# Attention mask in a diffusion block: from an added matmul to a product on VectorE, with the sums over keys one stage later

## The chip, the cores and the metric

The kernel runs on one core of a Trainium2 chip. The core has a matrix engine (TensorE, PE in the profile; its weight loads are PEld), three engines for elementwise work (VectorE or DVE, ScalarE or ACT, GpSimd or POOL) and a queue engine (SyncE or SP) that issues most DMAs here. TensorE writes to PSUM[...]; everything else lies in SBUF. The metric is the device time of one execution in microseconds; the time of the kernel before is the median of three runs.

## The reference

The input is x, 32 sequences of 256 tokens with 256 features, and a condition per sequence. A conditional state-space block is followed by two layers of attention and feed-forward, and the input is added at the end. The change concerns the attention alone:

```python
def local_attention(q, k, v):                      # WINDOW = 128, 8 heads of 64
    ...
    bk, bv = (look_around(bk), look_around(bv))    # each window also sees the one before
    sim = jnp.einsum('bhwid,bhwjd->bhwij', bq, bk)
    i = bt[:, :, None]
    j = btk[:, None, :]
    mask = (i < j) | (i > j + WINDOW) | (j == -1)
    sim = jnp.where(mask, -jnp.finfo(sim.dtype).max, sim)
    attn = jax.nn.softmax(sim, axis=-1)
    out = jnp.einsum('bhwij,bhwjd->bhwid', attn, bv)
```

So a query i sees the keys from i - 128 to i. For 256 tokens there are two windows of 128. Queries are l2-normalised and rotated before, as are keys; values are not.

## The kernel before

The 32 sequences go in four groups of eight. For each group a scan (the state-space block, `group_scan`) runs over 256 time steps, and two layers of attention and feed-forward follow. The scan of the first group runs alone. From then on the scan of the next group runs beside the two layers of the present one: `side_by_side` takes the attention and feed-forward as a sequence of pieces (each `yield` in `blocks` ends one) and gives out the 315 pieces of the scan evenly between them, about one and a half to a piece of attention. The last group has no scan beside it. Within this written order a scheduler settles the order on each engine; every engine then works in order, and semaphores tie the engines together.

The attention of one sequence is `blocks`' inner loop, eight pieces long. Sequence b is scored while sequence b+1 is already projected:

1. project v of the first window of b+1; turn (transpose) the second window of b
2. project q and k of the first window of b+1
3. `divide` b-1; scores of the second window's keys, all heads
4. scores of the first window's keys, half of the heads; project v of the second window of b+1
5. project q and k of the second window of b+1
6. scores of the first window's keys, the other half; output projection of b-1 (`finish`)
7. `sums` and `values` of b
8. turn of the first window of b+1

In the last two sequences of a layer, the pieces from the sixth on also carry the normalisation of the feed-forward's first input (`normalise`, `spread`).

A projection of q or k fills one PSUM bank (L736). `rotated` then works on it with all three elementwise engines: squares on ACT (L749), products with the rotation tables on DVE (L752, L757), sum of squares on DVE (L762, L766), the addition, the inverse root and the product with it on POOL (L760, L768, L769). `turn` transposes the result on TensorE (L775) and copies it with ACT (L780).

`scores` computes the transposed scores, keys on partitions. It fills two banks, one for the even and one for the odd heads. Each bank begins with a matmul that writes the mask into it (L934): the identity in bfloat16 times `mask_t`, which holds 0 where a key is seen and -32768 where not. The products of keys and queries (L941, 64 rows) accumulate onto it, and ACT takes the exponential of the whole bank (L950) into a tile `pT` of 128x512, of which six exist; a sequence uses all six. No maximum is subtracted.

`sums` adds the exponentials over the keys with a matmul per head (L960, `rs`), and DVE takes the reciprocal (L968). `values` multiplies with v (L979) and ACT copies the result (L986). `divide` spreads the reciprocal over the heads' rows by a matmul (L994), and DVE multiplies (L1002). `finish` is the output projection (L786), which DVE adds to the residual (L794).

All PSUM tiles but one come from one pool of seven banks (`ps_w`), taken in turn, so a matmul that opens a bank waits until the reader of that bank's former content is done. There is also a second program in the file (`exact`), for inputs whose scores might be too large; it isn't executed here.

Of the kernel before, what the change touches and what calls it, by code (L numbers as in the profile page):

```python
# [10 lines left out]
FP = mybir.dt.float32  # L11
BF = mybir.dt.bfloat16
I32 = mybir.dt.int32
AF = mybir.ActivationFunctionType
ALU = mybir.AluOpType
# [4 lines left out]
P = 128  # L20
# [18 lines left out]
W = 128  # L39
# [4 lines left out]
LN_EPS = 1e-5  # L44
CLIP = 10.0
MASKED = -1e30
MASKED_LOW = -32768.0


SCALES2 = 25.0  # L50
# [2 lines left out]
def bc(ap, axis, n):  # L53

    ap = ap.unsqueeze(axis)
    shape = list(ap.shape)
    shape[axis] = n
    return ap.broadcast_to(shape)
# [15 lines left out]
def kernel(  # L74
# [29 lines left out]
    nc = tc.nc  # L104
# [4 lines left out]
    const = ctx.enter_context(tc.tile_pool(name="const", bufs=1))  # L109
# [27 lines left out]
    ident = const.tile([P, P], FP, tag="ident", name="ident")  # L137
# [15 lines left out]
    for j in range(NJ):  # L153
# [18 lines left out]


    mask_t = const.tile([P, 2 * W], BF, tag="mask_t", name="mask_t")
    ident_b = const.tile([P, P], BF, tag="ident_b", name="ident_b")
    nc.vector.tensor_copy(ident_b, ident)
    nc.gpsimd.memset(mask_t, 0.0)
    nc.gpsimd.affine_select(
        out=mask_t[:, 0:W], in_=mask_t[:, 0:W], compare_op=ALU.is_ge, fill=MASKED_LOW,
        base=0, pattern=[[1, W]], channel_multiplier=-1,  # L180
    )
    nc.gpsimd.affine_select(
        out=mask_t[:, W : 2 * W], in_=mask_t[:, W : 2 * W], compare_op=ALU.is_ge,
        fill=MASKED_LOW, base=0, pattern=[[-1, W]], channel_multiplier=1,
    )


# [5 lines left out]
    for h in range(HEADS):  # L193
# [7 lines left out]
        out=b1g_sb[DH : DH + MREM], in_=b1[0:MREM, :, 1, len(MCH) - 1]  # L201
# [12 lines left out]
    with tc.tile_pool(name="setup", bufs=2) as setup, tc.tile_pool(  # L214
        name="setup_ps", bufs=2, space=PSUM
    ) as sps:

        for src, pos, dst in ((qk_scale, rot_c, rc_sb), (qk_scale_sw, rot_s, rs_sb)):
            tab = setup.tile([P, NW, 2, DH], FP, tag="tab", name="tab")
            nc.scalar.dma_start(out=tab, in_=pos)  # L220
            for l in range(L):
                sc = setup.tile([P, 2 * DH], FP, tag="qk_sc", name="qk_sc")
                nc.scalar.dma_start(
                    out=sc, in_=src[l].rearrange("a d -> (a d)").partition_broadcast(P)
# [39 lines left out]
        for i in range(3):  # L264
            for src, k, dst in ((wx_sb, 0, wsum), (wx0, 1, wbias)):
# [3 lines left out]
                for c in range(NC_):  # L269
# [4 lines left out]
                        start=(c == 0),  # L274
                        stop=(c == NC_ - 1),
# [12 lines left out]
    def program(ctx, exact):  # L288
# [10 lines left out]
        ps_w = ctx.enter_context(tc.tile_pool(name="psw", bufs=7, space=PSUM, reuse_waits="tile"))  # L299
# [496 lines left out]
        if exact:  # L796
# [4 lines left out]
                out=mask[:, 0:W], in_=mask[:, 0:W], compare_op=ALU.is_ge, fill=MASKED,  # L801
                base=0, pattern=[[1, W]], channel_multiplier=-1,
            )
            nc.gpsimd.affine_select(
                out=mask[:, W : 2 * W], in_=mask[:, W : 2 * W], compare_op=ALU.is_ge, fill=MASKED,
                base=0, pattern=[[-1, W]], channel_multiplier=1,
# [94 lines left out]
        class Attention:  # L901
# [24 lines left out]
            def scores(self, b, kw, i0, n):  # L926


                qT, kT, _ = self.qkv[b]
                nq = S - kw * W  # L930
                banks = []
                for r in range(2):
                    sc = ps_w.tile([P, n, nq], FP, tag="w", name="sc")
                    nc.tensor.matmul(  # L934
                        sc, ident_b, bc(mask_t[:, 0:nq], 1, n), start=True, stop=False
                    )
                    banks.append(sc)
                for i in range(n):
                    for r in range(2):
                        rows = slice(r * DH, (r + 1) * DH)  # L940
                        nc.tensor.matmul(  # L941
                            banks[r][:, i, :],
                            kT[rows, i0 + i, kw * W : (kw + 1) * W],
                            qT[rows, i0 + i, kw * W :],
                            start=False,
                            stop=(i == n - 1),
                        )
                for r in range(2):
                    p = aw.tile([P, n, nq], FP, tag="pT", name="pT", bufs=6)
                    nc.scalar.activation(p, banks[r], AF.Exp)  # L950
                    for i in range(n):
                        self.p[b, kw, i0 + i, r] = p[:, i, :]

# [192 lines left out]
        def ff_weights(l):  # L1146
            return (
                weights(w1, l, [P, KM, 2 * HID], "w1_sb"),
                weights(w2, l, [P, len(MCH), DM], "w2_sb"),
            )  # L1150
# [29 lines left out]
        def blocks(g, at, nxt):  # L1180

            for l in range(L):
                ff = FeedForward(g, l, at.res, *ff_weights(l))
                for b in range(GB):
                    more = b + 1 < GB
                    more and at.project(b + 1, 0, 2)
                    at.turn(b, 1)
                    yield
                    more and at.project(b + 1, 0, 0)
                    more and at.project(b + 1, 0, 1)  # L1190
                    yield
                    b > 0 and at.divide(b - 1)
                    at.scores(b, 1, 0, HEADS // 2)
                    yield
                    at.scores(b, 0, 0, 2)
                    more and at.project(b + 1, 1, 2)
                    yield
                    more and at.project(b + 1, 1, 0)
                    more and at.project(b + 1, 1, 1)
                    yield  # L1200
                    at.scores(b, 0, 2, 2)
                    b > 0 and at.finish(b - 1)
                    if b >= GB - 2:
                        ff.normalise(0, 2 * (b - GB + 2))
                    yield
                    at.sums(b)
                    at.values(b)
                    if b >= GB - 2:
                        ff.normalise(0, 2 * (b - GB + 2) + 1)
                        ff.spread(0, 2 * (b - GB + 2))  # L1210
                    yield
                    more and at.turn(b + 1, 0)
                    if b >= GB - 2:
                        ff.spread(0, 2 * (b - GB + 2) + 1)
                    yield
                yield
                at.divide(GB - 1)
                yield
                res, follow = at.res, None

                def last(m):
                    nonlocal follow
                    if m == 0:
                        if l + 1 < L:
                            follow = Attention(l + 1, res, *attention_weights(l + 1))
                        else:
                            follow = nxt()
                    if follow is not None:
                        lead_in(follow, m)

                pieces = feed_forward(ff, last)
                next(pieces)
                at.finish(GB - 1)
                yield
                for _ in pieces:
                    yield
                at = follow
            state_at[0] = at
# [3 lines left out]
        for _ in group_scan(0, ys):  # L1242
            pass
        at = Attention(
            0, [load_res(ys, j) for j in range(GB // 2)], *attention_weights(0)
        )
        for m in range(6):
            lead_in(at, m)
        for g in range(NG):
# [12 lines left out]
            at = state_at[0]  # L1262
# [119 lines left out]
```

## Time and profile before

| what | value |
|---|---|
| median of three runs | 4266.41 us (4258.27 to 4266.48) |
| the profiled execution, its own time | 4264.77 us |
| its span, first to last instruction | 4262.5 us |
| mean granted TensorE clock | 0.963 |
| DMA queue of most transfers | 34.1% of 16 engines' span |
| scan of the first group, alone | the first 546 us |
| mask matmuls (L934) | 384, of 128x512 bfloat16, mean 383 ns |
| exponentials (L950) | 384, of 128x512, mean 590 ns |
| sums over keys (L960) | 2048 instructions |
| reciprocal (L968) | 64, mean 1751 ns |

In the profile's lines an instruction is told by its line in the kernel, its engine and operation, and the tiles that it writes and reads (out<-in). A group's line gives the number of instructions, their busy time in us and the mean of one in ns, and then the idle time of the engine just before them, with what ended it. A line of waits gives the waiting instruction, what it waited for, the total in us, how often and the longest. Matmuls are pipelined, so that the busy time of one is longer than the distance from its start to the next one's start.

### The profile page before, as it was taken

The page shows a single profiled execution, that of the slowest core. Times are in us where ns is not written, and L with a number is a line of the kernel's source. Part 1 is how long each engine was busy: PE and PEld are TensorE (multiplying, and loading weights), DVE is VectorE, ACT ScalarE, POOL GpSimd, SP SyncE. Part 2 cuts the span into 40 slices and gives each one's busy share as a digit, 9 for nine tenths or more (in the row PEclk, how much of TensorE's full clock was granted, in tenths as well). Part 3 has the DMA queues.
Part 4 walks back from the last instruction along what each step waited for, and adds up shares of the span by engine and source line. Part 5 has one row for each costly group of instructions (what it writes and reads, how often), then busy time and mean ns, then how long its engine had stood idle before and what let it go on. Part 6 is the DMA issues. An engine that isn't in the chain of part 4 may idle for free. (4 is left out here: it accounts for less than half of the span.)

```text
span 4262.5 us, 51606 instructions
## 1 busy us (share of the span) xinstructions
PE 3885.2 (91%) x17980; PEld 2003.9 (47%) x17980; DVE 2600.1 (61%) x4952; ACT 1744.2 (41%) x3217; POOL 1684.0 (40%) x1749
## 2 busy tenths in 40 slices
PE   5777799898898999999899999999989899999999
PEld 2222255544455445544455445554455544654653
DVE  5777557666676546766776645766677653443442
ACT  2554335443444334443444423544344433322331
POOL 3333165323553156422555126532355314523531
PEclk9899999999999999999999999999999999999999
DMA  5777603443334312443433521344333431000000
GB/s 150 178 185 180 155 24 85 119 104 105 92 92 120 100 57 56 111 108 94 115 95 96 140 67 39 85 119 104 105 95 90 127 95 51 1 20 21 1 10 31
DMA packets 266114, 386.30 MB, mean 91 GB/s; under 512 B 161779, under 2 KB 170996, under 8 KB 263668
## 3 DMA queue, kind: packets, MB, share of 16 engines
q1 hardware_dynamic: 261776, 380.86, 34.1%
q8 instruction: 145, 2.38, 0.2%
q10 hardware_dynamic: 4068, 2.04, 0.2%
q14 instruction: 125, 1.02, 0.1%
HBM read 347.70 MB, written 33.55 MB: 89 GB/s over the span
## 5 line engine op out<-in xcount | busy, mean ns | idle before, releaser
L543 ACT ACTIVATE xrep<-xrep,beta 128x512 f32<-128x512 f32 x1024 | 693.1, 715 | 929.2 <-DMA xrep<-xnd 797.2
L550 DVE CUSTOM_DVE_ANT_0 h<-h,xrep,lim 128x512 f32<-128x512 f32 x1024 | 916.4, 895 | 149.7 <-ACT xrep L543 58.5
L736 PE MATMUL ps_qkv<-wqkv_sb,res 128*128 128x512 f32 x1536 | 733.6, 616 | 16.9 <-DMA res<-ys 6.3
L760 POOL TENSOR_TENSOR rot<-rot,swp 128x512 f32<-128x512 f32 x256 | 331.1, 1293 | 586.8 <-DVE swp L757 503.5
L736 PEld LDWEIGHTS ps_qkv<-wqkv_sb,res 128*128 128x128 f32 x1536 | 287.5, 196 | 359.4 <-issue 303.3
L562 PE MATMUL y<-h,ly 128*32 128x512 f32 x2048 | 411.3, 632 | 48.9 <-DVE h L550 48.0
L768 POOL TENSOR_TENSOR rn<-ss,neg_half 128x8 f32<-128x8 f32 x256 | 434.2, 1696 | 26.5 <-DVE ss L766 14.1
L1087 PE MATMUL po_f<-ag,w_sb 128*128 128x512 f32 (+1 forms) x768 | 378.8, 617 | 37.8 <-DVE ag L1076 37.8
L752 DVE TENSOR_TENSOR rot<-ps_qkv,rc_sb 128x512 f32<-128x512 f32 x256 | 175.6, 686 | 369.2 <-ACT sq L749 369.0
L326 PE MATMUL ps_in<-xg,w_in_sb 128*128 128x256 f32 x1024 | 393.0, 517 | 1.8 <-DMA xg<-in_xT_dram 1.5
L1066 PE MATMUL pa<-hT,w_sb 128*128 128x512 f32 (+1 forms) x896 | 363.8, 596 | 0.0
L1076 DVE SCALAR_TENSOR_TENSOR ag<-pa,b_sb,gl 128x512 f32<-128x512 f32 x192 | 143.4, 747 | 329.9 <-PE pa L1066 210.3
L1066 PE MATMUL pg<-hT,w_sb 128*128 128x512 f32 x640 | 313.7, 613 | 0.0
L769 POOL TENSOR_TENSOR rot<-rot,rn 128x512 f32<-128x512 f32 x256 | 276.7, 1081 | 19.1
L326 PEld LDWEIGHTS ps_in<-xg,w_in_sb 128*128 128x128 f32 x1024 | 190.1, 199 | 187.4 <-issue 127.1
L1029 POOL TENSOR_TENSOR rstd<-ve,neg_half 128x1 f32<-128x1 f32 x128 | 76.5, 598 | 508.1 <-DVE ve L1027 494.5
L373 DVE SCALAR_TENSOR_TENSOR acc<-xr,wc_sb,acc 128x256 f32<-128x256 f32 x384 | 190.0, 506 | 126.7 <-POOL acc L362 122.7
L1087 PEld LDWEIGHTS po_f<-ag,w_sb 128*128 128x128 f32 (+1 forms) x768 | 141.6, 194 | 229.4 <-issue 143.6
L950 ACT ACTIVATE pT<-sc 128x512 f32<-128x512 f32 x384 | 206.2, 590 | 97.1 <-PE sc L941 96.4
L786 PE MATMUL ps_wo<-oT,wo_sb 128*128 128x256 f32 x1024 | 237.3, 385 | 0.0
L583 POOL TENSOR_TENSOR xd<-xd,dskip_sb 128x512 f32<-128x512 f32 x64 | 86.8, 1357 | 367.1 <-DMA xd<-xnd 202.4
L749 ACT ACTIVATE sq<-ps_qkv 128x512 f32<-128x512 f32 x256 | 148.9, 594 | 200.7 <-PE ps_qkv L736 147.5
(144 smaller groups left out, 5444.2 us busy)
## 6 DMA issues: line engine op xcount, KB each, us to landing
xrep<-xnd SPq DMA_DIRECT2D x512, 512.0 KB
xnd<-xn SPq DMA_DIRECT2D x64, 256.0 KB
xd<-xnd SPq DMA_DIRECT2D x256, 64.0 KB
wqkv_sb<-in_wqkv_dram SPq DMA_DIRECT2D x8, 1536.0 KB
w_sb<-in_w_dram SPq DMA_DIRECT2D x8, 1364.0 KB
xg<-in_xT_dram SPq DMA_DIRECT2D x64, 128.0 KB
ys<-yo SPq DMA_DIRECT2D x64, 128.0 KB
res<-ys SPq DMA_DIRECT2D x32, 256.0 KB
```

Of the source, the lines that this page charges most:

```text
L326: nc.tensor.matmul(ps, w_in_sb[:, k, ch * P : (ch + 1) * P], x, start=(k == 0), stop=(k == KM - 1),)
L543: nc.scalar.activation(bx, bx, AF.Copy, scale=ck[c]["beta"][:, t : t + 1])
L550: nc.vector._custom_dve(TENSOR_ADD_SAT, out=h_new, in0=state["h"], in1=bx, s0=ck[c]["lim"][:, 0, t : t + 1], s1=ck[c]["lim"][:, 1, t : t + 1],
L562: nc.tensor.matmul(ck[c]["y", hb][32 * q : 32 * q + 32, :], ly[hb % 2][:, 32 * t : 32 * t + 32], ck[c].pop(("h", hb * TB + t)), start=(i = ...
L736: nc.tensor.matmul(ps, res[b // 2][:, k, b % 2, t0 : t0 + W], wqkv_sb[:, k, a * DI : (a + 1) * DI], start=(k == 0), stop=(k == KM - 1),)
L760: nc.gpsimd.tensor_add(rot, rot, swp)
L768: nc.gpsimd.tensor_tensor(rn, ss, neg_half, ALU.pow)
L769: nc.gpsimd.tensor_mul(rot, rot, bc(rn, 2, DH))
L786: nc.tensor.matmul(po[:, d], wo_sb[:, c, d * P : (d + 1) * P], oT[:, c, :], start=(c == 0), stop=(c == NC_ - 1),)
L950: nc.scalar.activation(p, banks[r], AF.Exp)
L1066: nc.tensor.matmul(ps[0:n, :], self.w1[:, k, half_ * HID + o : half_ * HID + o + n], self.h[j][:, k].rearrange("p b t -> p (b t)"), start= ...
L1087: nc.tensor.matmul(self.po[d], self.w2[0:n, m, d * P : (d + 1) * P], self.ag[m][0:n, :], start=(m == 0), stop=(m == len(MCH) - 1),)
```

## The change

The mask is no longer added to the scores. `mask_t` now holds 1 where a key is seen and 0 where not. The products of keys and queries open their banks themselves, ACT takes the exponential of the unmasked scores, and DVE multiplies each tile `pT` in place with the mask, spread over the heads. The identity in bfloat16 and the copy that made it are gone. In `blocks`, the turn of the next sequence's first window moves ahead of `sums` and `values`, which come one piece later; the pieces of `normalise` and `spread` stay where they were.

```diff
     mask_t = const.tile([P, 2 * W], BF, tag="mask_t", name="mask_t")
-    ident_b = const.tile([P, P], BF, tag="ident_b", name="ident_b")
-    nc.vector.tensor_copy(ident_b, ident)
-    nc.gpsimd.memset(mask_t, 0.0)
+    nc.gpsimd.memset(mask_t, 1.0)
     nc.gpsimd.affine_select(
-        out=mask_t[:, 0:W], in_=mask_t[:, 0:W], compare_op=ALU.is_ge, fill=MASKED_LOW,
+        out=mask_t[:, 0:W], in_=mask_t[:, 0:W], compare_op=ALU.is_ge, fill=0.0,
...
                 for r in range(2):
-                    sc = ps_w.tile([P, n, nq], FP, tag="w", name="sc")
-                    nc.tensor.matmul(
-                        sc, ident_b, bc(mask_t[:, 0:nq], 1, n), start=True, stop=False
-                    )
-                    banks.append(sc)
+                    banks.append(ps_w.tile([P, n, nq], FP, tag="w", name="sc"))
                 for i in range(n):
                     for r in range(2):
                         rows = slice(r * DH, (r + 1) * DH)
@@
                             qT[rows, i0 + i, kw * W :],
-                            start=False,
-                            stop=(i == n - 1),
+                            start=True,
+                            stop=True,
                         )
                 for r in range(2):
                     p = aw.tile([P, n, nq], FP, tag="pT", name="pT", bufs=6)
                     nc.scalar.activation(p, banks[r], AF.Exp)
+                    nc.vector.tensor_mul(p, p, bc(mask_t[:, 0:nq], 1, n))
                     for i in range(n):
                         self.p[b, kw, i0 + i, r] = p[:, i, :]
@@
                     if b >= GB - 2:
                         ff.normalise(0, 2 * (b - GB + 2))
                     yield
-                    at.sums(b)
-                    at.values(b)
+                    more and at.turn(b + 1, 0)
                     if b >= GB - 2:
                         ff.normalise(0, 2 * (b - GB + 2) + 1)
                         ff.spread(0, 2 * (b - GB + 2))
                     yield
-                    more and at.turn(b + 1, 0)
+                    at.sums(b)
+                    at.values(b)
                     if b >= GB - 2:
                         ff.spread(0, 2 * (b - GB + 2) + 1)
                     yield
```

## The prediction

> **What bounds the kernel now.** I read the engine shares, then the windows by stage, TensorE's timeline where nothing else interferes, and last the groups and waits.
>
> ```profile
> PE 3885.2 (91%) x17980; PEld 2003.9 (47%) x17980; DVE 2600.1 (61%) x4952; ACT 1744.2 (41%) x3217; POOL 1684.0 (40%) x1749
> ```
>
> TensorE (PE) is busy for 91% of the span, VectorE (DVE) for 61%. The windows split this by stage (length, then busy time of each engine):
>
> ```profile
> core 0: us, PE busy (x) PEld busy (x) DVE busy (x) ACT busy (x) POOL busy (x), PEclk, DMA share, GB/s
> ...
> 546.00:819.00 273.00, 253.75 (x1533) 150.80 (x1532) 186.98 (x361) 125.18 (x238) 156.07 (x155) 0.99 0.27 73
> ...
> 1053.00:1377.00 324.00, 288.90 (x1688) 165.09 (x1686) 222.88 (x410) 149.58 (x285) 161.27 (x151) 0.96 0.39 99
> ...
> 3576.00:3778.00 202.00, 197.53 (x1278) 122.73 (x1277) 97.34 (x186) 79.20 (x142) 111.75 (x88) 0.99 0.03 9
> ```
>
> The first two are the attention of layer 0 and layer 1 beside the next group's scan. Such a pair comes three times, 48 sequences in all. The third is attention in the last group, with no scan beside it. That happens twice, for 16 sequences. With the scan, DVE is busy for 68 to 69% of the window and PE for 89 to 93%. Without it DVE has 48% and PE 98%. There PE's timeline repeats every 26.6 us:
>
> ```profile
> start us, us, engine line op out<-in xcount [idle before <-releaser]
> 3705.19 1.46 PE L994 MATMUL rb<-rinv,head_rows 128*128 128x256 f32 x6
> 3706.48 0.59 PE L934 MATMUL sc<-mask_t,ident_b 128*128 128x512 bf16 x2
> 3707.01 1.16 PE L941 MATMUL sc<-qT,kT 64*128 64x128 f32 x16
> 3708.10 0.61 PE L934 MATMUL sc<-mask_t,ident_b 128*128 128x512 bf16 x2
> 3708.64 1.14 PE L941 MATMUL sc<-qT,kT 64*128 64x256 f32 x8
> ```
>
> No row shows idle time before it: each pair of mask matmuls holds PE for 0.53 us from its start to the next row's start. Next the waits: what PE waits for in the whole span, then what DVE waits for in the layer 1 window (total, times, longest).
>
> ```profile
> PE tp_hn L1044 <- DVE hn L1031: 51.3, 28, 4.6
> PE rs L960 <- ACT pT L950: 49.1, 20, 8.5
> ...
> PE sc L934 <- DVE swp L757: 19.0, 17, 1.8
> ```
>
> ```profile
> DVE acc L373 <- POOL acc L362: 20.9, 10, 6.1
> DVE sg L593 <- ACT th_g L587: 20.0, 8, 5.6
> DVE rot L752 <- ACT sq L749: 13.3, 8, 3.1
> DVE hn L1031 <- POOL rstd L1029: 12.0, 4, 5.7
> ```
>
> PE's own waits in attention are few, and most name DVE or the exponentials. DVE, when idle, waits as often for POOL's round trips (acc, hn) as for PE's products (rot).
>
> **What the Trainium skill says.** "Perfetto Trace Analysis", Identifying the Most-Contended Engine, warns that matmul busy time is no fair measure of how near TensorE is to its limit. I therefore use starts of successive matmuls, not busy time. "TensorE: Matmul & The Clock Gate", Back-to-back issue gap, gives N/2.4 + 2.5 ns, or 216 ns for 512 columns. The first mask matmul of a pair is followed after 0.214 us here, so the trace agrees. "VectorE: DVE Perf Modes", The TRN2 errata, gives (N+151)/0.96 ns for an fp32 tensor_tensor, or 691 ns at 512 elements. The nearest row here, with one operand in PSUM, has 0.68 us. "SBUF — State Buffer", Who interferes with whom, says that a DVE instruction with two SBUF inputs contends with a GpSimd instruction that reads SBUF. The trace fits that: the scan step (two SBUF inputs) has a median of 0.81 us but a mean of 0.895, with single ones of 1.88. The new multiply is of this kind.
>
> **The change part by part.**
>
> *Mask matmuls removed.* 384 of them, in 192 pairs. The unmerged records show 0.214 us after the first of a pair and 0.308 after the second. The extra 0.09 is the step to the 64-row products, and it stays, because it will follow whatever matmul comes before. So a pair saves 0.43 us: 192 x 0.43 = 82.6 us, or 1.29 us per sequence. In the last group that is a plain gain, 16 x 1.29 = 21 us. In the 48 others (62 us) it counts only as far as PE still sets the pace.
>
> *Multiplies added.* 384 on DVE, each 128x512 with both inputs in SBUF. These bound one from below and above:
>
> ```profile
> L550 DVE CUSTOM_DVE_ANT_0 h<-h,xrep,lim 128x512 f32<-128x512 f32 x1024 | 916.4, 895 | 149.7 <-ACT xrep L543 58.5 <-PE y L562 40.1 <-DVE h L550 13.1
> ...
> L1002 DVE TENSOR_TENSOR oT<-oT,rb 128x512 f32<-128x512 f32 x128 | 86.7, 678 | 21.4 <-PE rb L994 19.0 <-ACT kT L780 2.4
> ```
>
> From below, the oT product has 0.68 us, of which neighbours overlap by 0.08, so 0.60. From above, the scan step's mean of 0.895. I take 0.70, the skill's figure plus a little contention: 269 us in all, 4.2 per sequence. DVE goes to about (187 + 34)/273 = 81% and (223 + 34)/324 = 79% in the two scan windows, and to 65% in the last group. In the last group its idle time, half the stage, covers the multiplies. With the scan only part is covered. Each multiply waits for its exponential, and behind it on DVE stand the next scan steps, the convolution, the gate, the residual sum and the reciprocal. PE waits for those through banks (swp 19.0, in other rows rinv 9.3, qkv on swp 5.1, oT 4.8) and through hn (51.3): 90 us in all. Bounds: no growth if the idle 31% covers everything. If waits grow like busy over idle (72 to 85% in a scan sequence: 2.6 to 5.7), 90 us becomes 195, or +105. I take half of the present sum again: +45.
>
> *Sums and values one stage later.* Before, PE waits 49.1 us for exponentials at the sums (73.5 counted by weight loads, which partly hide). Now the turn of the next sequence (8 transposes, 0.87 us) stands in between, and beside the scan mostly one or two scan pieces of 0.9 to 1.9 us too: about 2.5 us more cover. Against it stand two multiplies, 1.4 us, behind two rotation chains of about 2.3 us on DVE. In the last group DVE ends those chains 0.7 us after the second exponential, the multiplies would end at about 3719.9, and the sums start at 3720.2: no stall. With the scan I expect half of the 49.1 to go: -25. Bounds: -49, or 0 if DVE's queue replaces ACT's.
>
> *What moves with it, at nothing.* The turn needs POOL's rotated tiles. In the last group POOL has these 6.7 us before the sums' present start, which covers the earlier place; without that cover it would cost POOL's lateness, up to 3.6 us a time as in the present waits on rot. Its two ACT copies (0.59 us each) now precede the copies of values, with no DMA and nothing on SP or POOL moved. The reciprocal comes one stage later, but 2.75 us of value products and at least 5.2 of projections still stand ahead of its use. In the last two sequences of a layer one normalisation loses the cover of sums and values (1.44 + 2.75 us) and its neighbour gains it: even, within 8 us. The pT tiles live longer, yet all six are still freed before the next sequence's scores.
>
> *Sum.* -83 - 25 + 45 = -63. The profiled execution took 4264.8 us (span 4262.5), 1.6 below the median of 4266.4. So 4202 for it, 4203 against the median; I say 4205.
>
> **The rivals.**
>
> *DVE keeps up wholly* (0.20). All of PE's saving comes through and the sums stop waiting: 83 + 40 less 10 of new waits = -113, so 4153. For it: 31% idle DVE. Against it: DVE idles at points, in order, and can't be late for free.
>
> *Gain eaten, no change within 0.2%* (0.10). New DVE waits of 83 to 115 us, just inside the upper bound: 4258 to 4275.
>
> *DVE becomes the pace beside the scan: slower* (0.24). Its place is the six scan windows. If DVE's waits for POOL and ACT do not shrink when it has more to do, a window takes its busy time, plus these waits, plus 48 multiplies. In layer 1 the waits are 57 (acc, hn, stat, rhs, xc, h) and 20 (sg): 223 + 77 + 48 x 0.8 = 338 against 324. In layer 0 all waits but those on PE's products (rot, res, st) are 51: 187 + 51 + 38 = 276 against 273. Three times 14 and 3 is +51; less 21 in the last group +30, so 4296. With 0.895 a multiply it is +57, 4323. It decides from about 0.7 us a multiply if no wait shrinks. Against it: waits such as acc on POOL shrink when something else is placed in them, and the built order does place multiplies between the rotation chains and the convolution.
>
> That the mask matmuls do not really leave is no rival: the built order has no mask matmul, and 384 multiplies.
>
> **How the numbers follow.** My forecast, part of the gain survives, has 0.46, with its own range 4170 to 4240. The other cases have 0.20, 0.10 and 0.24. A measurement of this kernel tells about 0.2% from no change (the runs before spread by that): 8.5 us. Faster is 0.46 + 0.20, same 0.10, slower 0.24. The range that leaves out one in ten on each side reaches from 4148 (best case with a little more) to 4290 (a bit over half of the slow case).
>
> **What would show it.** Right: no mask rows; in the last group a sequence every 25.3 us instead of 26.6; multiplies of 0.65 to 0.8 us; waits of the sums below 49 us and naming DVE; waits on hn and swp up by some tens of us. Wrong: layer 1 windows as long as before or longer, with PE waiting for DVE at sums, y or banks; multiplies near 0.9 us; POOL's rotations much longer than their present 1.29 and 1.08 us, which would make the turns wait.

## The result, and the profile after

The changed kernel takes 4262.97 us (median of four, 4251.46 to 4268.31) against 4263.86 for the kernel before, measured beside it (4258.27 to 4266.48). The ratio is 0.9996, with a 95% interval of 0.9972 to 1.002. The forecast was 4205 and faster. What came is the rival with the lowest chance: the gain is eaten.

The profiled execution took 4268.31 us, its span is 4266.6. The page's engine line of the changed kernel:

```profile
PE 3842.9 (90%) x17596; PEld 1996.5 (47%) x17596; DVE 2907.0 (68%) x5335; ACT 1743.3 (41%) x3217; POOL 1762.5 (41%) x1749
```

The 384 mask matmuls are gone, and VectorE is busy for 307 us more. GpSimd, to which the change gives nothing, is busy for 78 us more. The windows of the changed kernel, cut from a layer's first scores to the first scores of its eighth sequence (layer 0 and layer 1 beside the scan), and seven sequences and a bit of the last group:

```profile
core 0: us, PE busy (x) PEld busy (x) DVE busy (x) ACT busy (x) POOL busy (x), PEclk, DMA share, GB/s
547.40:799.90 252.50, 223.34 (x1293) 133.16 (x1292) 202.31 (x365) 105.81 (x203) 156.10 (x146) 0.95 0.22 61
1071.40:1363.00 291.60, 259.38 (x1471) 149.00 (x1470) 241.23 (x420) 136.35 (x255) 165.94 (x145) 0.94 0.38 99
3591.00:3790.00 199.00, 189.57 (x1238) 120.09 (x1237) 135.74 (x235) 78.55 (x144) 119.88 (x89) 0.98 0.03 11
```

The same stretch of layer 0 took 236.7 us before and takes 252.5 now; that of layer 1 took 290.3 and takes 291.6; that of the last group's first layer took 183.2 and takes 177.8. Over whole layers (from first scores to first scores) the three layer-0 passes together grew by 37 us, the three of layer 1 shrank by 19 and the last group by 15. That this stretch of layer 1 is as long as before is what the prediction named as a sign against it. Of the 16 us in layer 0's stretch some 10 come with the new order alone (246.3 us in the first experiment below), and the rest of that layer gives 8 of them back; whole layers are the safer measure. VectorE is now at 80% and 83% of the scan windows (forecast 81 and 79).

The last group did what was forecast, and a little more. Its TensorE timeline in the changed kernel:

```profile
start us, us, engine line op out<-in xcount [idle before <-releaser]
3696.41 2.03 PE L934 MATMUL sc<-qT,kT 64*128 64x128 f32 x24
3698.37 5.42 PE L733 MATMUL ps_qkv<-wqkv_sb,res 128*128 128x512 f32 x12
...
3709.30 1.51 PE L954 MATMUL rs<-pT,head_cols 128*32 128x256 f32 x32
3710.74 2.82 PE L973 MATMUL ov<-pT,v_sb 128*64 128x256 f32 x32
...
3721.44 2.03 PE L934 MATMUL sc<-qT,kT 64*128 64x128 f32 x24
```

A sequence comes every 25.03 us (3696.41 to 3721.44) instead of 26.6, and no row of that steady stretch shows idle time. That is 0.5 us for each pair of mask matmuls, where the prediction took 0.43. The multiplies and the sums one stage later cost nothing there.

Now the multiply's own rows: the page's group line, then the tile view's counts and durations (minimum, median, maximum in ns):

```profile
L944 DVE TENSOR_TENSOR pT<-pT,mask_t 128x512 f32<-128x512 f32 x384 | 314.3, 854 | 36.2 <-ACT pT L943 36.1
```

```profile
L944 DVE TENSOR_TENSOR pT<-pT,mask_t x384: 658/683/1785, 550.1 to 4119.6; 128x512 f32<-128x512 f32 x192
```

The median is 683 ns, near the 691 that the prediction started from, but the mean is 854. The multiplies fall into two kinds: 282 of the 384 take 0.70 us or less, and 98 take 0.8 to 1.8. What GpSimd does at the time goes far to tell them apart. Of the 64 that start while it is in its product with the rotation (L757, 128x512), 55 are long, and the mean of the 64 is 1227 ns. The 88 that are overlapped by nothing but its inverse root on tiles of 128x8 (L765) have a mean of 682, the 44 that nothing of GpSimd overlaps 683. GpSimd pays too: its products with the rotation (L757, L766) rose from 1293 and 1081 ns to 1376 and 1119, and an L757 that a multiply overlaps has a mean of 1514, one without 1298. The Trainium skill, "SBUF — State Buffer", Who interferes with whom, states that a VectorE instruction with two SBUF inputs contends with a GpSimd instruction that reads SBUF. For the large products the trace agrees; beside the small one it shows no slowing.

The waits of TensorE in the whole span of the changed kernel (total us, times, longest; rows that changed little are left out):

```profile
...
PE sc L934 <- DVE swp L754: 48.1, 30, 3.3
...
PE tp_hn L1038 <- DVE mv L1019: 31.6, 5, 7.7
PE rs L954 <- DVE pT L944: 29.6, 25, 2.9
PE tp_hn L1038 <- DVE hn L1025: 27.6, 8, 7.2
...
PE tp_hn L1038 <- DVE ve L433: 13.4, 3, 4.7
```

Against the kernel before: the sums' wait for exponentials (49.1) has become 29.6 for the multiply; the scores' wait for a bank that VectorE frees went from 19.0 to 48.1; the turn of the normalised input (tp_hn) from 51.3 to 72.6 (31.6 + 27.6 + 13.4). All of TensorE's waits together grew by about 50 us.

Last the clock. The mean granted TensorE clock fell from 0.963 to 0.950. Windows of the changed kernel, one clock record (3.41 us) each, around one wait in layer 1, and the timeline there:

```profile
core 0: us, PE busy (x), PEclk, DMA share, GB/s
1297.05:1300.46 3.41, 2.38 (x30) 1.00 0.55 153
1300.46:1303.88 3.42, 1.20 (x5) 1.00 0.01 1
1303.88:1307.29 3.41, 3.41 (x7) 0.50 0.20 70
1307.29:1310.70 3.41, 3.41 (x14) 1.00 0.36 84
```

```profile
1302.68 1.13 PE L323 MATMUL ps_in<-xg,w_in_sb 128*128 128x256 f32 x4 [3.25 <-DVE res L791]
1303.64 3.38 PE L733 MATMUL ps_qkv<-wqkv_sb,res 128*128 128x512 f32 x4
1306.82 1.28 PE L772 MATMUL tr_qk<-ident,rot 128*128 128x128 f32 x8
```

TensorE waits 3.25 us for VectorE's residual sum. The record that holds most of this wait has 1.20 us of work; in the next record the clock is 0.50, and four projections take 3.18 us up to the next row's start. In the last group, where the clock is full, the same row of four takes 1.82 (3713.49 to 3715.31). So a wait is paid twice: once as idle time and again as slow work behind it, which costs up to 1.7 us in a record (half of 3.41). Many slow stretches are longer than one record: after the first scores they last 5.8 us in the mean.

To add this up, I split the time from the first scores to the end of the span into three: idle time (gaps that the profile counts as waits of TensorE), clock loss (half of the time at clock 0.5 in which TensorE is not idle), and the rest, which is TensorE's work at full clock, with gaps of less than 0.15 us, which aren't counted as waits.

| kernel | first scores to end | idle | clock loss | rest |
|---|---|---|---|---|
| before | 3715.9 | 226.3 | 91.2 | 3398.4 |
| after | 3719.2 | 276.7 | 127.1 | 3315.4 |
| difference | +3 | +50 | +36 | -83 |

TensorE's work fell by 83 us, the forecast's 82.6. The agreement is closer than the split is sharp: kernels below with the same matmuls as the changed one have a rest between 3302 and 3338. Waits and their slow clock took all of it back. Most of both lies in layer 0 beside the scan, where idle time grew by 37 us and clock loss by 31. The experiments ask which part of the change brought them.

### The profile page after: what moved, and what is told of

It reads as the page before. It is cut to its first block, busy times and chain, and to the rows that moved or that the text cites. A ratio compares the mean times of both kernels' runs of the same rounds, so it can differ in the third digit from the quotient of the medians.

```text
span 4266.6 us, 51214 instructions
## 1 busy us (share of the span) xinstructions
PE 3842.9 (90%) x17596; PEld 1996.5 (47%) x17596; DVE 2907.0 (68%) x5335; ACT 1743.3 (41%) x3217; POOL 1762.5 (41%) x1749
## 5 line engine op out<-in xcount | busy, mean ns | idle before, releaser
L733 PE MATMUL ps_qkv<-wqkv_sb,res 128*128 128x512 f32 x1536 | 750.9, 628 | 19.1 <-DVE swp L754 9.2
L757 POOL TENSOR_TENSOR rot<-rot,swp 128x512 f32<-128x512 f32 x256 | 352.1, 1376 | 560.1 <-DVE swp L754 501.7
L765 POOL TENSOR_TENSOR rn<-ss,neg_half 128x8 f32<-128x8 f32 x256 | 458.1, 1790 | 27.0 <-DVE ss L763 15.2
L944 DVE TENSOR_TENSOR pT<-pT,mask_t 128x512 f32<-128x512 f32 x384 | 314.3, 854 | 36.2 <-ACT pT L943 36.1
L766 POOL TENSOR_TENSOR rot<-rot,rn 128x512 f32<-128x512 f32 x256 | 286.4, 1119 | 19.8
L934 PE MATMUL sc<-qT,kT 64*128 64x128 f32 (+1 forms) x2048 | 240.5, 349 | 55.4 <-DVE swp L754 48.1
```

The lines of the kernel that those rows point to most:

```text
L733: nc.tensor.matmul(ps, res[b // 2][:, k, b % 2, t0 : t0 + W], wqkv_sb[:, k, a * DI : (a + 1) * DI], start=(k == 0), stop=(k == KM - 1),)
L757: nc.gpsimd.tensor_add(rot, rot, swp)
L765: nc.gpsimd.tensor_tensor(rn, ss, neg_half, ALU.pow)
L766: nc.gpsimd.tensor_mul(rot, rot, bc(rn, 2, DH))
L934: nc.tensor.matmul(banks[r][:, i, :], kT[rows, i0 + i, kw * W : (kw + 1) * W], qT[rows, i0 + i, kw * W :], start=True, stop=True,)
L944: nc.vector.tensor_mul(p, p, bc(mask_t[:, 0:nq], 1, n))
```

## The experiments

The texts on record name theories by letters. A: the multiply's new waits eat what mask matmuls and order gain. B: the new order is what costs. C: a TensorE with fewer matmuls is granted a lower clock, and that is what costs. Diffs are against the changed kernel unless said otherwise; every kernel ran beside the kernel before (4262.3 to 4263.6 us in these comparisons).

**The new order alone.** The kernel before, with nothing but the order changed:

```diff
-                    at.sums(b)
-                    at.values(b)
+                    more and at.turn(b + 1, 0)
...
-                    more and at.turn(b + 1, 0)
+                    at.sums(b)
+                    at.values(b)
```

> The kernel before with the order alone changed: sums and values one piece later, turn one piece earlier, mask still by matmul, no multiply. Theory A (DVE's multiplies eat what PE saves): the order alone gives PE more cover for the exponentials, waits of the sums fall from 49 us to below 20, and the time is 4225 to 4255. Theory B (the new order is what costs: normalisations at the end of a layer, turns, sums that meet the next projections): 4275 to 4320, with the sixth and seventh sequence of each layer longer by 4 to 14 us as in the changed kernel. Theory C (a sparser TensorE gets a lower clock): clock as before, 0.96.

Measured: 4248.63 us (4244.35 to 4253.44), ratio 0.9965 (0.9952 to 0.9977). The order gains 14 us by itself, as A had it; the sums' wait for exponentials fell from 49.1 to 20.6, just short of A's 20. B falls.

**The old order with the multiply.** The same edit undone in the changed kernel:

```diff
-                    more and at.turn(b + 1, 0)
+                    at.sums(b)
+                    at.values(b)
...
-                    at.sums(b)
-                    at.values(b)
+                    more and at.turn(b + 1, 0)
```

> The changed kernel with the old order: mask as DVE's multiply, no mask matmul, sums and values where they were. Theory A: the multiplies now have one piece less of cover, so the sums wait for them; 4290 to 4340, and waits of the sums on the multiply over 100 us. Theory B: faster than the changed kernel, 4190 to 4240. Theory C: clock 0.95 as in the changed kernel, time about 4263 to 4290.

Measured: 4304.93 us (4300.67 to 4310.48), ratio 1.0097 (1.008 to 1.0114), as A had it; C named the clock rightly (0.95), but not the time. With the multiply in place the new order is worth 42 us (4305 less 4263). What it covers stands in this kernel's waits of TensorE:

```profile
PE rs L954 <- DVE pT L944: 113.2, 61, 5.5
```

Without the later stage the sums wait 113 us for the multiply; with it 29.6.

**No mask at all.** The multiply is left out, so the scores aren't masked.

```diff
                     nc.scalar.activation(p, banks[r], AF.Exp)
-                    nc.vector.tensor_mul(p, p, bc(mask_t[:, 0:nq], 1, n))
```

> The changed kernel without the multiply: no mask at all is applied, so the attention of this kernel sees all keys of the two windows. PE has the changed kernel's work and order, DVE has that of before. Theory A: the whole saving of PE shows, 4150 to 4190, clock back at 0.96 or more, in both scan windows shorter by 10 us or more than in the changed kernel. Theory B: 4250 to 4300, since the order is still there. Theory C: clock stays at 0.95 because PE still has fewer matmuls, and no more than 30 us are gained, 4230 to 4265.

Measured: 4200.02 us (4197.83 to 4203.86), ratio 0.9853 (0.9836 to 0.9869), ten above A's range and far from the others. The clock is 0.956 to 0.958, where A had 0.96 or more and C 0.95. Against the changed kernel, the multiply costs 63 us. Against the new order alone (4249), the removal of the mask matmuls brings 49, not 83. Taken in this sequence, the steps of the change are -14 for the order, -49 for the mask matmuls and +63 for the multiply.

Where did the other 34 us of the mask matmuls go? Layer by layer, this kernel gains 24 us on the order-alone kernel in the last group, 19 in layer 1 (12 of it in attention) and, in layer 0, 4: layer 0 beside the scan takes the same time with no mask in any form as in the kernel before (1525 us in three passes, and 1527). In the split, layer 0 has 28 us less work than with the order alone, but 8 us more idle time and 16 us more clock loss: most of what is freed there goes to the slow clock. (The two profiled executions also differ by 5.5 us before the first scores, where the kernels are alike.)

**Both.** The mask matmuls put back beside the multiply, with a stationary operand of zeros, so that they cost time and change nothing:

```diff
+    zero_b = const.tile([P, P], BF, tag="zero_b", name="zero_b")
+    nc.gpsimd.memset(zero_b, 0.0)
...
-                    banks.append(ps_w.tile([P, n, nq], FP, tag="w", name="sc"))
+                    sc = ps_w.tile([P, n, nq], FP, tag="w", name="sc")
+                    nc.tensor.matmul(
+                        sc, zero_b, bc(mask_t[:, 0:nq], 1, n), start=True, stop=False
+                    )
+                    banks.append(sc)
...
-                            start=True,
-                            stop=True,
+                            start=False,
+                            stop=(i == n - 1),
```

> The changed kernel with 384 idle matmuls put back where the mask matmuls were (a stationary tile of zeros, so they add nothing); the multiply masks. PE has the work of before, DVE that of the changed kernel. Theory A: beside the scan DVE is the pace, so PE's 62 us there cost only part: 4285 to 4320, the last group longer by 21 us. If PE were still the pace everywhere, 4263 + 83 = 4346. Theory C: the clock rises towards 0.96 because PE is denser, and the time is near 4263 to 4290.

Measured: 4330.21 us (4324.98 to 4335.16), ratio 1.0156 (1.0139 to 1.0173), between A's range and the case in which TensorE is the pace everywhere. The last group is 29 us longer than in the changed kernel, where 21 were expected. The matmuls cost 67 us here, and the multiply 82 (4330 less 4249). C falls as the main cause: its times were 4263 to 4290 here and 4230 to 4265 with no mask, and with the matmuls back the clock is hardly higher (0.953 to 0.955, against 0.950 to 0.953). A part of it stays: with no mask the clock loss is 110 us, with the order alone 96.

So the multiply is what costs, at 63 to 82 us. Five runs ask why: its length, its engine, or its place.

**A shorter operation in the same place.** The multiply by the mask becomes one by 1.0, in place, with a single input; no mask is applied.

```diff
-                    nc.vector.tensor_mul(p, p, bc(mask_t[:, 0:nq], 1, n))
+                    nc.vector.tensor_scalar(p, p, 1.0, None, ALU.mult)
```

> The changed kernel with the multiply by the mask replaced by a multiply with 1.0 in the same place, so no mask is applied: the same wait for the exponential, the same readers, but one input in SBUF instead of two, and a shorter instruction (0.3 to 0.5 us expected instead of 0.854 on the average). Theory A1, the length of the multiplies is what costs: about half of the 63 us that the multiply costs come back, 4225 to 4245, and half of the growth in PE's waits and in time at half clock. Theory A2, the place in DVE's queue and the wait for ACT cost, not the length: 4250 to 4265.

```profile
L944 DVE TENSOR_SCALAR pT<-pT x384: 393/419/1546, 548.8 to 4091.5; 128x512 f32<-128x512 f32 x192
```

Measured: 4245.32 us (4240.86 to 4246.82), ratio 0.9959 (0.9945 to 0.9973). This is 0.3 us above what the theory of length expected, and below the range of the other. The operation has a median of 419 ns and a mean of 539, and still costs 45 us over no mask. Length and second input together make 18 of the 63.

**On GpSimd.** The same product on another engine:

```diff
-                    nc.vector.tensor_mul(p, p, bc(mask_t[:, 0:nq], 1, n))
+                    nc.gpsimd.tensor_mul(p, p, bc(mask_t[:, 0:nq], 1, n))
```

> The changed kernel with the multiply on POOL instead of DVE. Theory A, DVE's queue is what PE waits for: DVE is back at the load of before, waits on banks (swp) and normalisations fall, and if POOL can bear 384 more instructions of 1.3 to 1.7 us (40% to 53% busy) the time is 4205 to 4245. Rival: POOL's in-order queue takes DVE's part, rotations come late and the turns and sums wait for POOL; 4280 to 4360.

Measured: 4545.52 us (4544.61 to 4551.89), ratio 1.0669 (1.0651 to 1.0687), far beyond the rival's range. The group line of the product and the waits of TensorE in this kernel:

```profile
L944 POOL TENSOR_TENSOR pT<-pT,mask_t 128x512 f32<-128x512 f32 x384 | 457.7, 1209 | 29.6 <-ACT pT L943 29.4
```

```profile
PE rs L954 <- POOL pT L944: 149.8, 68, 5.6
```

It takes VectorE's load away completely (VectorE is at 59%), and yet is much the slowest of all. With 1209 ns a product, the sums wait for it five times as long as in the changed kernel; TensorE's idle time is 467 us (190 more, of which all waits at the sums make 158) and the clock loss 208. A free VectorE is no help if the sums wait for a slower engine.

**The load without the place, first try.** Instead of the multiply, VectorE makes a reduction of 128x512 over a constant, whose result nobody reads; no mask.

```diff
-                    nc.vector.tensor_mul(p, p, bc(mask_t[:, 0:nq], 1, n))
+                    idle = aw.tile([P, HEADS], FP, tag="idle", name="idle", bufs=2)
+                    nc.vector.tensor_reduce(idle, head_rows, AX.X, ALU.add)
```

> The order of after, no mask matmul and no mask at all (scores go unmasked into the exponential); in place of the multiply VectorE makes a reduction over another 128x512 tile in SBUF, whose result nobody reads, so that VectorE carries a load of about 0.68 us a pair that neither waits for the exponential nor stands between it and the sums. Theory A, VectorE's load alone costs the time: 4240 to 4262 us, near the half-length run and after. Theory B, what costs is the multiply's place behind the exponential and ahead of the sums: 4200 to 4230, near the run without a mask.

```profile
L945 DVE TENSOR_REDUCE idle<-head_rows x384: 622/676/685, 38.6 to 1121.2; 128x8 f32<-128x512 f32 x192
```

Measured: 4218.98 us (4215.26 to 4220.47), ratio 0.9892 (0.9875 to 0.9908). The number fits B of that text, but the tile view shows that the run doesn't test it: the last reduction starts at 1121.2 us. As they depend on nothing, the scheduler put all 384 into the first quarter; 14 of the 19 us are lost before the first scores, which come at 560.6 us instead of 546.7. Inconclusive.

**The load tied to its sequence.** The reduction reads the sequence's turned queries and keys instead; no mask.

```diff
-                    nc.vector.tensor_mul(p, p, bc(mask_t[:, 0:nq], 1, n))
+                    idle = aw.tile([P, HEADS // 2], FP, tag="idle", name="idle", bufs=2)
+                    nc.vector.tensor_reduce(
+                        idle, (qT, kT)[r][:, :, kw * W : (kw + 1) * W], AX.X, ALU.add
+                    )
```

> As the load-only run (order of after, no mask matmul, no mask, an idle reduction of 128x512 on VectorE for each multiply), but the reduction now reads the sequence's own turned queries or keys, so that it can't be made far ahead of its sequence. It doesn't wait for the exponential, and no sum waits for it. If load alone is what costs, 4240 to 4262 us; if the multiply's place in the chain is what costs, 4200 to 4220, near the run without a mask (4200).

**The load on the exponential.** The reduction reads `p` itself, right after the exponential, where the multiply stands; but it doesn't write `p`, so no sum waits for it. No mask either.

```diff
-                    nc.vector.tensor_mul(p, p, bc(mask_t[:, 0:nq], 1, n))
+                    idle = aw.tile([P, n], FP, tag="idle", name="idle", bufs=2)
+                    nc.vector.tensor_reduce(idle, p, AX.X, ALU.add)
```

> The same, but the reduction reads the exponentials: VectorE waits for ScalarE in the same place as the multiply does, while the sums do not wait for VectorE. No mask is applied. If what costs is that VectorE's queue stands still behind an exponential, 4225 to 4255 us, above the tied load; if it is the longer chain exponential, multiply, sums, as the tied load within 8 us.

The tied load: 4248.96 us (4242.92 to 4255.73), ratio 0.9971 (0.9961 to 0.9981). The load on the exponential: 4193.57 us (4185.12 to 4197.51), ratio 0.9835 (0.9819 to 0.9852), under every figure expected of it. The two tile views, of the tied load and then of the load on the exponential, with VectorE's idle time ahead of the reductions:

```profile
L945 DVE TENSOR_REDUCE idle<-qT x192: 648/678/689, 534.0 to 4093.0; 128x4 f32<-128x512 f32 x192
L945 DVE TENSOR_REDUCE idle<-kT x192: 648/676/686, 538.4 to 4093.6; 128x4 f32<-128x512 f32 x192
its engine sat idle before it (us, times) until:
  ACT qT L777: 140.8, 46
  ACT kT L777: 20.0, 10
```

```profile
L945 DVE TENSOR_REDUCE idle<-pT x384: 653/675/690, 550.2 to 4047.4; 128x2 f32<-128x512 f32 x128, 128x4 f32<-128x512 f32 x64
...
its engine sat idle before it (us, times) until:
  ACT pT L943: 36.9, 32
```

Both spread 384 operations of 0.68 us over the whole kernel. Behind the exponential they cost nothing that can be told from no mask at all (4194 against 4200; the intervals overlap), although VectorE waits for exponentials as long there (36.9 us) as before the multiplies (36.1). So 384 operations of 0.68 us on VectorE need not cost anything, and neither need its standing still behind an exponential. With the tied load alone I would have concluded the opposite: at 4249 it fits the theory of load, and it costs 49 us though no sum waits for it. There VectorE stands idle for 161 us ahead of the reductions, which wait for ScalarE's copies of queries and keys; that this is its whole cost of 49 us was not tested apart.

What is left, as the likeliest reading, is the chain exponential, product, sums. Here are TensorE's waits at the sums, first with no product in the chain (the load on the exponential), then with the shorter operation in it:

```profile
PE rs L955 <- ACT pT L943: 4.8, 3, 2.1
```

```profile
PE rs L954 <- DVE pT L944: 19.3, 14, 2.4
```

In the changed kernel the sums wait 29.6 us for the product, with the old order 113.2. The scores' wait for a bank, which rose from 19.0 to 48.1 with the change, isn't for the product's sake. With no mask it is 36.6, and with the load on the exponential, the fastest run of all, it is as long as with the multiply:

```profile
PE sc L934 <- DVE swp L754: 49.1, 32, 3.3
```

In the three-way split:

| kernel | us, median | idle | clock loss | rest |
|---|---|---|---|---|
| no mask | 4200.0 | 232.2 | 109.8 | 3309.1 |
| load on the exponential | 4193.6 | 227.3 | 119.0 | 3301.9 |
| shorter operation, sums wait | 4245.3 | 261.3 | 116.1 | 3315.6 |
| the changed kernel | 4263.0 | 276.7 | 127.1 | 3315.4 |
| tied load | 4249.0 | 263.8 | 128.5 | 3308.8 |

From the second row to the third, a shorter operation with the same number of inputs costs 52 us more when the sums need its result. The profiled executions are 43 us apart, and 34 of these are idle time: all waits at the sums grow by 21, those at the value products by 9, those at the normalised input by 14, and others shrink. From the third row to the fourth, the longer operation with two inputs adds 18.

This is not yet proof that the dependence is the whole cause. With another dependence the scheduler also settles another order on the engines, and that wasn't held fixed; the tied load shows that an operation can cost as much without any sum behind it. A rival is the contention with GpSimd: GpSimd is busy for 1689 us with no mask, 1692 with the load on the exponential, 1723 with the shorter operation and 1762 with the multiply, so it slows where the time is lost. Against this rival, TensorE's waits for GpSimd hardly move (28, 24, 25 and 34 us), and the tied load leaves GpSimd as it was (1694) and still costs 49. No run has a product that the sums need and that leaves GpSimd alone.

**The last two sequences in the old order.** In the changed kernel, sums and values of the last two sequences of a layer come before the turn again, with the normalisations in their old cover.

```diff
-                    more and at.turn(b + 1, 0)
-                    if b >= GB - 2:
+                    late = b < GB - 2
+                    if late:
+                        more and at.turn(b + 1, 0)
+                    else:
+                        at.sums(b)
+                        at.values(b)
...
-                    at.sums(b)
-                    at.values(b)
+                    if late:
+                        at.sums(b)
+                        at.values(b)
+                    else:
+                        more and at.turn(b + 1, 0)
```

> The changed kernel, but the last two sequences of each layer in the old order, so that sums and values again cover the first of two normalisations. If the normalisations that lost their cover matter (waits on hn and mv are 4 to 5 us longer in a layer than before): 4230 to 4252. If they only swap places, or the sums now wait for the multiplies in these sequences: 4255 to 4275.

Measured: 4261.61 us (4255.51 to 4273.36), ratio 0.9997 (0.9985 to 1.0009): the same as the changed kernel. Its wait for the normalised input is one row:

```profile
PE tp_hn L1038 <- DVE hn L1025: 39.4, 21, 4.2
```

39.4 us instead of 72.6, while the wait of the sums rises from 31 to 49. With the multiply in place the normalisations had lost cover, and giving it back moved about half of the wait to the sums, with no gain in time.

**Mixed: each form where it is cheaper.** The new order everywhere; mask matmuls in the first three groups, the multiply in the last group, where nothing runs beside it. One VectorE operation turns the mask's values into 1 and 0 ahead of the last group. The diff is against the kernel before, and shows only its main lines.

```diff
...
+                    if not self.product:
+                        nc.tensor.matmul(
+                            sc, ident_b, bc(mask_t[:, 0:nq], 1, n), start=True, stop=False
+                        )
...
+                    if self.product:
+                        nc.vector.tensor_mul(p, p, bc(mask_t[:, 0:nq], 1, n))
...
+                    if g + 1 == NG - 1:
+                        nc.vector.tensor_scalar(
+                            mask_t, mask_t, -1.0 / MASKED_LOW, 1.0, ALU.mult, ALU.add
+                        )
```

> The new order everywhere; mask by matmul in the three groups that have the scan beside them, by DVE's multiply in the last group alone, where the mask tile is turned into ones and zeros by one instruction. If the gain lies where I read it, the last group (16 sequences) keeps the 15 us by which it was shorter in the changed kernel and the rest keeps the time of the kernel with the order alone: 4249 - 15 = 4234, between 4225 and 4242. If the order alone already holds all of the gain: 4245 to 4252.

Measured: 4232.75 us (4229.68 to 4238.58), ratio 0.9931 (0.9914 to 0.9948). This is inside the range expected. It beats both kernels, by about 31 us: 14 for the order and 16 more, which the last group gives.

**Mixed, with the old order in layer 0.** As the mixed kernel, but sums and values come before the turn in layer 0 beside the scan. The edit of the order is that of the old tail, with another condition:

```diff
...
+                    late = l > 0 or g == NG - 1
...
```

> The mixed kernel (mask matmul in the first three groups, multiply in the last) with the old order of sums and values in layer 0, beside the scan, and the new order elsewhere. If the new order costs beside the scan and gains elsewhere, about 3 us less for each of the three layer-0 groups: 4218 to 4228. If the order is even beside the scan: 4228 to 4238, as the mixed kernel.

Measured: 4228.58 us (4226.14 to 4231.63), ratio 0.9914 (0.9897 to 0.9931), on the border of the two ranges. The seven sequences' stretches of layer 0 are back at 237 to 241 us, from 246 to 248, but the rest of those layers takes 269 to 275 instead of 265. The three whole layers together gain 7 us; against the mixed kernel the intervals overlap, so the difference stays undecided.

## Why the prediction was wrong

**Mask matmuls removed (-82.6).** As work, right: the rest of the split fell by 83.0 us. As time, wrong: 49 without the multiply, 67 with it. The step itself said that the 62 us beside the scan count only as far as TensorE is the pace there, and the sum then took all of them. Without the multiply, layer 0 gave 4 of its 31. In the last group the saving was sized a little low: 0.52 us a pair, which is the whole distance of 0.53 before, so the 0.09 us that the step took as staying didn't stay.

**Multiplies added (+45 of waits).** From no mask to the changed kernel, idle grew by 44.5 us. That the number fits is luck, since it was half of a sum of waits taken again. The reason given was VectorE's load (busy over idle) and the work that stands behind a waiting multiply. As many operations of 0.68 us in the same place, with the same waits for ScalarE, cost nothing, so these two alone aren't enough. Most of the cost comes when the sums need the result, and a smaller part with length; how far the order that the scheduler then settles takes part stays open. The duration was sized low: 0.854 us in the mean, inside the bounds of 0.60 to 0.895. The "little contention" of the estimate is a doubling for a quarter of the multiplies (98 of 384, 1.36 us in the mean) and none for most others.

**Sums and values one stage later (-25).** Right in sign, and near in the sums' own wait, which fell by 22 us in all (53.7 to 31.3); as time, -14 without the multiply and -42 with it. That the two interact, so that most of the stage's cover goes to the multiply, was in the text, and not in the number.

**What moves with it, at nothing.** For the normalisations "even, within 8 us" holds for the order alone (50.9 us of waits, from 51.3), but with the multiply it came out as +21. By the run with the old tail it isn't a cost of its own, since the time is the same when it is taken back. Not in the step was that GpSimd would get slower, which the prediction had only as a sign of being wrong; the turns' wait for it stayed (24.0 and 25.6 us).

**Sum (-63).** This is the step that failed. It added work saved and waits gained at full clock. Measured: work -83, waits +50 where the sum had +20, and a third term that the sum does not have, +36 for the slow clock after the waits. The 66 us between forecast and result in the profiled runs are these 30 and 36. The profile before already showed the term: its clock was 0.963, and 91 us of its time after the first scores were lost so.

**The rivals.** "Gain eaten" named the right outcome, with 83 to 115 us of new waits. What was measured is 50 us of waits, net of what the order saved, and 36 of clock, 86 in all; so over a third of what ate the gain was the clock, which this rival doesn't have either. Its own sum doesn't close either: with the order's -25 such waits give 4241 to 4273, not 4258 to 4275. "VectorE becomes the pace beside the scan" has support in its place (layer 0 grew) and against it in its mechanism: with 384 reductions behind the exponential VectorE carries as many operations as with the multiplies, at 0.68 us against 0.85, and nothing is lost. The slower kernel that it expected, at 4296, did not come. "VectorE keeps up wholly" at 4153 falls; even with no mask and no load the time is 4200. One line was misread: the rot row of VectorE's waits names ScalarE's squares (sq), not TensorE's products.

## What to carry to other kernels

Time freed on the busiest engine is a gain only where that engine sets the pace; read it stage by stage, and price each new wait of TensorE with the slow clock that follows it. What an added operation costs depends on its place more than on its engine's load: 384 reductions of one size cost nothing behind the exponentials and 49 us behind the turned queries and keys. Ask first what it waits for, who needs its result, and how soon. Where stages have different limits, use each form where it is cheap, as the mixed kernel does.

## What the runs showed of the hardware

The clock fell to half after stretches that were only partly idle. In the kernel before, the clock drops 41 times after the first scores, and in the record of 3.41 us ahead of a drop TensorE was idle for 2.28 us in the mean (0.9 at the least). In the changed kernel it is 53 drops, after 2.37 us (0.7 at the least). It isn't a sharp threshold: 37 and 40 records with over 1 us of idle time brought no drop. The Trainium skill, "TensorE: Matmul & The Clock Gate", HAM oscillation — how this bites in real kernels, gives as the rule that TensorE should have no gaps of over about 3.4 us. Here gaps of 1 to 3 us, single or summed within a record, were enough: ahead of 28 of the 41 drops and 36 of the 53 no single gap was as long as 3.4 us. The measurement decides.

A product of 128x512 with both inputs in SBUF (one fp32, one bfloat16) took 683 ns on VectorE with GpSimd quiet, 1227 in the mean when it started inside a GpSimd product of 128x512, and 1158 in the median on GpSimd itself.
